# A fused convolution, Fourier mixing and FFN kernel: parts of the convolution and of the FFN issued in other stages of the mixing

## The chip, the cores and the metric

The kernel runs on one core of one Trainium2 chip, as one program. The metric is the device time of one execution in microseconds; less is better. Three executions of the kernel before took 10711.68, 10723.89 and 10726.16 us, so its median is 10723.89 us.

The core has five engines, each with its own queue that it works off in order: TensorE (PE in the profile, with PEld for the loading of weights), VectorE (DVE), ScalarE (ACT), GpSimd (POOL) and SyncE (SP, which here only starts transfers). They meet through semaphores: an instruction that needs another engine's result waits at the head of its queue, and everything behind it waits too.

## The reference, cut to what matters

The input is 64 images of 96 channels and 56x56 pixels in fp32. Three parts follow each other.

```
# 1 convolution block, per image
out = silu(bn(expand_w @ x))                 # 1x1, 96 -> 192 channels
out = channel_shuffle(shift_groups(out))     # shifts by one pixel, a quarter of the channels each way
out = silu(merge_bn(bn(depthwise3x3(out)) + bn(out * id_w)))
se  = sigmoid(grouped(relu(grouped(mean(out)))))      # squeeze and excitation, one gate per channel
x   = silu(bn(proj_w @ (out * se)) + x)               # 1x1, 192 -> 96
# 2 mixing, t = x as 3136 tokens of 96
h = relu(bn(layernorm(t) @ w1.T))            # 96 -> 192
X = fft(h, axis=tokens)
xr, xi = relu(X.re*rd - X.im*id + rb), relu(X.im*rd + X.re*id + ib)
t = t + bn(ifft(xr + 1j*xi).real @ w2.T)
# 3 FFN; q_mul rounds to a float with 5 exponent and 2 mantissa bits, q_acc to 5 and 10 bits
h = relu(q_acc(q_acc(q_mul(layernorm(t)) @ q_mul(W1)) + q_mul(b1)))   # 96 -> 384
t = t + q_acc(q_acc(q_mul(h) @ q_mul(W2)) + q_mul(b2))
```

## The kernel before, in words

Everything of an image stays in on-chip memory; an image is 96 channels on partitions (two blocks of 48 with a gap, 112 in all) by 3136 pixels. The loop at the end of the kernel (L668 to L683) runs over images b. For each it drains one generator, `mixing(b)`, and beside it two others: `ffn(b - 1)` for the image before and `conv_block(b + 1)` for the next. The schedule is written by hand: each generator issues some instructions and yields a weight, and `weave` (L651) advances the side generators so that they have used a share of their total cost as large as the share of the main one (`ffn` up to 0.85 of it, `conv_block` over all of it). So instructions stand in every engine's queue in the order in which `weave` called for them.

The parts, by the name of the PSUM tile that a reader finds in the profile:

- `expand_a`, `expand_b` (L268, L278): 1x1 expansion on PE into ps_ea and ps_eb, SiLU on ACT into e_a (128 channels, 7 parts) and e_b (the other 64 as two half images on 128 partitions, 5 parts).
- `depthwise` (L301): nine taps on DVE, each one instruction over 128x1568 elements (L307 the first, L309 the other eight), three calls for a picture: two halves of e_a and one of e_b. They accumulate in d, a tile with a single buffer. Then SiLU on ACT with a sum (L328), the gate (L339 to L357: small matmuls ps_se, Relu, Tanh, and scaled projection weights pw), and the projection (L363 to L368): eight parts of three matmuls into ps_pj, SiLU on ACT into t. Last it loads the image after the next (L371).
- `deviations` (L374): the mixing's layernorm. Seven times ps_c, squares on ACT, ps_v, a scaling on DVE (L395) and a power of -1/2 on POOL (L396); two `spread`s (L398) turn the deviation into a row that is written into t by DMA, and the factors into rs_full. In `mixing` they come first and nothing of the mixing can run before them.
- `mixing` (L414), after that: ps_w1 (L435, eight groups, evacuated by DVE at L444), ps_f1 (L459, six groups, copied by ACT at L468), ps_f2 (L487 and L493, six groups; each needs two ACT instructions L507, four DVE instructions L508 and L509, a Relu on ACT L510 and `mirrored` on DVE L570), ps_w2 (L523, L524, four groups, ACT L527), ps_i1 (L537, three groups, ACT L544) and ps_i2 (L555, four groups, added to t by DVE at L565). These PSUM tiles share two buffers (pool psa); all the other PSUM tiles share four (psb).
- `ffn` (L575): seven `centre` steps (ps_n L586, squares on ACT L588, a sum and scaling on DVE L591 and L592, the power on POOL L593), each followed by `turn` (DVE xt L599, which waits for the power, then ps_x L604 and an fp8 copy on ACT L605); then 21 `hidden` steps (ps_h L612, ACT copy to fp16 L614, bias on DVE L615, cast to fp8 on POOL L616) and seven `result` steps (ps_o L623, ACT copy L625, DVE L626, POOL adds t L628, SP writes the output L630).

t has two buffers, so image b + 1's projection writes the buffer from which `ffn(b - 1)` reads; x, with its own two buffers, is read by the expansion and by the projection.

Of the kernel before, what the change touches and what calls it, by code (L numbers as in the profile page):

```python
# [16 lines left out]
HW = 56  # L17
# [5 lines left out]
RPC = 8  # L23
# [11 lines left out]
def conv_attn_ffn(  # L35
# [265 lines left out]
    def depthwise(dst, e, r0, h):  # L301
        for n, tap in enumerate((4, 0, 1, 2, 3, 5, 6, 7, 8)):
            dy, dx = divmod(tap, 3)
            win = e[:, dy + r0 : dy + r0 + HH, dx : dx + HW]
            w = taps[:, h, tap : tap + 1]
            if n == 0:
                nc.vector.tensor_scalar(dst, win, w, None, ALU.mult)  # L307
            else:
                nc.vector.scalar_tensor_tensor(dst, win, w, dst, ALU.mult, ALU.add)  # L309
            yield 1.8 if n else 1.0  # L310

    def together(main, side):

        for w in main:
            yield w + next(side, 0.0)
        yield from side

    def conv_block(b):
        xi = x_buf[b % 2]
        tv = t_buf[b % 2][:, 0:NPIX].rearrange("p (b a) -> p b a", a=HW)  # L320

        d = work.tile([128, 3 * HH, HW], F32, tag="wide", name="d", bufs=1)
        sums = small.tile([128, 3], F32, tag="sums", name="sums")

        def mid_silu(i):
            dst = d[:, i * HH : (i + 1) * HH, :]
            h = i // 2
            nc.scalar.activation(dst, dst, AF.Silu, bias=mid_b[:, h : h + 1], accum_out=sums[:, i : i + 1])  # L328

        yield from together(depthwise(d[:, 0:HH], e_a, 0, 0), expand_b(b))  # L330
        mid_silu(0)
        yield from depthwise(d[:, HH:HW], e_a, HH, 0)
        mid_silu(1)
        yield from together(
            depthwise(d[:, HW : 3 * HH], e_b, 0, 1), expand_a(b + 1) if b + 1 < NB else iter(())
        )
        mid_silu(2)
        yield 2.0
# [10 lines left out]
        for h in range(2):  # L349
            nc.tensor.matmul(ps[:, h : h + 1], lhsT=ep_w[:, h, :], rhs=red, start=True, stop=True)  # L350
        for h in range(2):

            nc.scalar.activation(gate[:, h : h + 1], ps[:, h : h + 1], AF.Tanh, bias=ep_bh[:, h : h + 1], scale=0.5)
        nc.vector.tensor_scalar(gate, gate, 0.5, 0.5, ALU.mult, ALU.add)
        pw = small.tile([128, 3, CP], F32, tag="pw", name="pw", bufs=1)
        nc.vector.tensor_scalar(pw[:, 0, :], pj_w[:, 0, :], gate[:, 0:1], None, ALU.mult)
        nc.vector.tensor_scalar(pw[:, 1:3, :], pj_w[:, 1:3, :], gate[:, 1:2], None, ALU.mult)  # L357
        yield 1.0
        for j in range(HW // PJ):
# [4 lines left out]
            nc.tensor.matmul(ps, lhsT=pw[:, 0, :], rhs=d[:, r0 : r0 + PJ, :], start=False, stop=False)  # L364
            nc.tensor.matmul(  # L365
                ps, lhsT=pw[:, 1 + half, :], rhs=d[:, HW + rb : HW + rb + PJ, :], start=False, stop=True
            )
            nc.scalar.activation(tv[:, :, r0 : r0 + PJ], ps.rearrange("p a b -> p b a"), AF.Silu, bias=pj_sh)  # L368
            yield 0.5
# [4 lines left out]
    def deviations(b):  # L374
# [37 lines left out]
        return squares, variances, spread  # L412

    def mixing(b):  # L414
        t = t_buf[b % 2]
        squares, variances, spread = deviations(b)
# [9 lines left out]
        yield 1.5  # L426

        for g, (d, j0, n) in enumerate(
# [13 lines left out]
            if g == 0:  # L442
                spread(16, 12)
# [8 lines left out]
            yield 0.15 * n  # L452

        for g in range(C // 16):
# [17 lines left out]
            yield 2.0  # L472

        last = None
        for par, pq, k0, n in (
# [38 lines left out]
            yield 1.2  # L514
        mirrored(*last)

        for k0 in range(0, NK, 8):
# [10 lines left out]
            yield 3.0  # L528

        for g in range(3):  # L530
# [14 lines left out]
            yield 2.5  # L545

        for g in range(4):
# [18 lines left out]
            yield 1.0  # L566
# [8 lines left out]
    def ffn(b):  # L575
# [5 lines left out]
        def centre(g):  # L581
# [6 lines left out]
            nc.scalar.activation(sq, cen[:, :, 0:C], AF.Square)  # L588
            v = small.tile([CP, 4], F32, tag="v2", name="v2")
# [6 lines left out]
        def turn(g):  # L596
            cen, rs = held.pop(g)
# [3 lines left out]
            )  # L601
            ps = psb.tile([C, 8, HW], F32, tag="psb", name="ps_x")
# [4 lines left out]
        def hidden(j, m):  # L607
# [7 lines left out]
            nc.vector.tensor_scalar(y16, y16, qb1[:, m : m + 1], 0.0, ALU.add, ALU.max)  # L615
            nc.gpsimd.tensor_copy(held[j][:, m, :], y16, saturate=False)  # L616

        def result(j):
            h8 = held.pop(j)
            rows = slice(j * RPC, (j + 1) * RPC)  # L620
# [4 lines left out]
            nc.scalar.copy(o16, ps.rearrange("p (a b) -> p a b", b=HW))  # L625
            nc.vector.tensor_scalar(o16, o16, qb2, None, ALU.add)  # L626
# [8 lines left out]
        for g in range(NJ // 4 + 1):  # L635
            if g < NJ // 4:
                centre(g)
                yield 0.7
            if g:
                turn(g - 1)  # L640
                yield 0.6
        for j in range(NCH + 1):
            for m in range(3):
                if j < NCH:
                    hidden(j, m)
                    yield 0.4
                if m == 1 and j:
                    result(j - 1)
                    yield 0.3

    def weave(main, total, sides):  # L651
# [3 lines left out]
        for w in main:  # L655
            at += w / total
            for i, (side, cost, lo, hi) in enumerate(sides):
                goal = cost * min(1.0, (at - lo) / (hi - lo))
                while done[i] < goal:
                    step = next(side, None)  # L660
                    done[i] = cost if step is None else done[i] + step
# [5 lines left out]

    with tc.manual_schedule():  # L668
        if NB > 1:
            load_x(1)  # L670
        for _ in expand_a(0):
            pass
        for _ in conv_block(0):
            pass
        for b in range(NB):
            sides = []
            if b:
                sides.append((ffn(b - 1), 19.6, 0.0, 0.85))
# [174 lines left out]
```

## Time and profile before

| | |
|---|---|
| median of three runs | 10723.89 us |
| the profiled execution's own time | 10724.89 us |
| its span, first to last instruction | 10723.1 us |
| instructions | 262959 |
| mean granted TensorE clock | 0.856 of full speed |
| read from and written to HBM | 82.67 MB and 77.07 MB, 15 GB/s |

The profile was taken by the hardware on one execution. A group line gives the line of the code, the engine, the operation, tiles written and read with their shape, the number of instructions, their busy time in us and the mean of one in ns, and the idle time of the engine just before them with what ended it. A line of waits reads: engine and waiting line, what released it, then the total in us, how often, and the longest. A line of the timeline gives start and duration in us, the instruction, and in brackets the idle time before it. Matmuls overlap in PE, so a busy PE is not one at its peak; an fp32 matmul appears as two instructions. The granted clock (PEclk) is 1.00 at full speed and 0.5 at half; a mean lies between. The depthwise taps are the costliest DVE work, and the POOL casts of the FFN cost it most time:

```profile
L309 DVE SCALAR_TENSOR_TENSOR d<-e_a,taps,d 128x1568 f32<-128x1568 f32 x1024 | 1907.0, 1862 | 0.7
L616 POOL CAST h<-y 128x448 fp8e5<-128x448 f16 x1344 | 1589.4, 1193 | 1992.4 <-DVE y L615 1972.7
```

### The profile page before, as it was taken

What the parts mean: (1) busy time and instruction counts of PE and PEld (TensorE: products, weight loads), DVE (VectorE), ACT (ScalarE), POOL (GpSimd) and SP (SyncE); (2) the same over time, 40 slices, a digit from 0 to 9 for tenths busy, and PEclk for the clock granted to TensorE, in tenths of its full rate; (3) what the DMA queues carried; (4) which work ended last, traced back from release to release, by engine and by line L of the source; (5) the groups of instructions that cost most, each with busy time, mean ns of one, the idle gap of its engine ahead of it and who ended that gap; (6) DMA issues with size and microseconds to landing.
All of it is one profiled execution on the core that took longest, in us unless ns stands there. A gap on an engine that the chain in (4) does not pass through costs nothing. (4 is left out here: it accounts for less than half of the span.)

```text
span 10723.1 us, 262959 instructions
## 1 busy us (share of the span) xinstructions
PE 8726.5 (81%) x118530; PEld 6595.5 (62%) x118530; DVE 6560.7 (61%) x9035; ACT 4142.9 (39%) x7691; POOL 4211.8 (39%) x2704
## 2 busy tenths in 40 slices
PE   6888888888888888888888888887888888888787
PEld 4666666666666666665666656666666566666665
DVE  6656566566565665655656656566565565665655
ACT  2334344343343433433434334344343343433433
POOL 1444344344443344433433444334443443344433
PEclk8888888888888888888888888888888888888887
DMA  2110110101101111011010110111101101011000
GB/s 38 13 18 15 16 19 13 17 15 16 19 15 16 18 13 18 15 16 19 13 17 15 16 18 14 16 18 13 18 15 16 19 13 17 15 16 18 15 11 15
DMA packets 411392, 177.45 MB, mean 17 GB/s; under 512 B 366194, under 2 KB 409706, under 8 KB 410010
## 3 DMA queue, kind: packets, MB, share of 16 engines
q1 hardware_dynamic: 408508, 155.59, 11.6%
q8 instruction: 930, 15.24, 0.6%
q10 hardware_dynamic: 1264, 3.53, 0.1%
q0 software_dynamic: 496, 1.50, 0.1%
q14 instruction: 194, 1.59, 0.1%
HBM read 82.67 MB, written 77.07 MB: 15 GB/s over the span
## 5 line engine op out<-in xcount | busy, mean ns | idle before, releaser
L593 POOL TENSOR_TENSOR rs<-v,mhalf 112x4 f32<-112x4 f32 x448 | 987.3, 2204 | 3802.6 <-DVE v L592 3600.6
L616 POOL CAST h<-y 128x448 fp8e5<-128x448 f16 x1344 | 1589.4, 1193 | 1992.4 <-DVE y L615 1972.7
L309 DVE SCALAR_TENSOR_TENSOR d<-e_a,taps,d 128x1568 f32<-128x1568 f32 x1024 | 1907.0, 1862 | 0.7
L487 PE MATMUL ps_f<-l_tab,buf_g 128*128 128x112 f32 x3712 | 667.2, 353 | 605.4 <-DVE ue L509 604.7
L628 POOL TENSOR_TENSOR o<-t,o 112x448 f32<-112x448 f32 x448 | 941.6, 2102 | 430.6 <-DVE o L626 333.3
L309 DVE SCALAR_TENSOR_TENSOR d<-e_b,taps,d 128x1568 f32<-128x1568 f32 x512 | 1070.0, 2090 | 5.0
L487 PEld LDWEIGHTS ps_f<-l_tab,buf_g 128*128 128x128 f32 x3712 | 616.2, 258 | 705.9 <-issue 693.1
L435 PE MATMUL ps_w<-w1c,t 112*64 112x96 f32 x14336 | 1029.3, 327 | 3.2 <-DMA t<-dev_t 1.7
L435 PEld LDWEIGHTS ps_w<-w1c,t 112*64 112x64 f32 x14336 | 955.5, 197 | 40.9 <-issue 21.6
L591 DVE TENSOR_REDUCE v<-sq 112x4 f32<-112x384 f32 x448 | 247.0, 551 | 1177.8 <-ACT sq L588 1177.7
L523 PE MATMUL ps_w<-w2a,buf_h 128*112 128x96 f32 x3712 | 785.9, 299 | 144.6 <-DVE ue L509 144.6
L615 DVE TENSOR_SCALAR y<-y,qb 128x448 f16<-128x448 f16 x1344 | 646.9, 496 | 397.7 <-ACT y L614 384.1
L459 PE MATMUL ps_f<-f_tab,buf_h 128*64 128x58 f32 x24576 | 800.3, 224 | 81.5 <-DVE buf_h L444 81.5
L459 PEld LDWEIGHTS ps_f<-f_tab,buf_h 128*64 128x64 f32 x24576 | 749.8, 138 | 159.6 <-DVE buf_h L444 91.9
L523 PEld LDWEIGHTS ps_w<-w2a,buf_h 128*112 128x112 f32 x3712 | 610.1, 209 | 334.9 <-issue 226.6
L396 POOL TENSOR_TENSOR rs<-v,mhalf 112x4 f32<-112x4 f32 x448 | 705.8, 1579 | 253.8 <-DVE v L395 247.3
L368 ACT ACTIVATE t<-ps_pj,pjbn_b 112x392 f32<-112x392 f32 x512 | 316.5, 618 | 1241.3 <-PE ps_pj L365 1241.3
L524 PE MATMUL ps_w<-w2b,buf_h 128*112 128x96 f32 x3712 | 760.9, 292 | 0.0
L565 DVE SCALAR_TENSOR_TENSOR t<-ps_i,bn2c_b,t 112x392 f32<-112x392 f32 x512 | 296.7, 621 | 742.0 <-PE ps_i L555 742.0
L605 ACT CAST xq<-ps_x 96x448 fp8e5<-96x448 f32 x448 | 238.0, 531 | 1260.2 <-PE ps_x L604 1260.2
L623 PE MATMUL ps_o<-h,q 128*112 128x448 fp8e5 x1344 | 449.1, 428 | 317.6 <-POOL h L616 314.8
L444 DVE SCALAR_TENSOR_TENSOR buf_h<-ps_w,rs_full 128x768 f32<-128x768 f32 (+1 forms) x512 | 436.9, 854 | 423.4 <-PE ps_w L435 423.3
(159 smaller groups left out, 15841.9 us busy)
## 6 DMA issues: line engine op xcount, KB each, us to landing
x<-in_x SPq DMA_DIRECT2D x128, 588.0 KB, 8.4
out_dram<-o SPq DMA_DIRECT2D x896, 84.0 KB, 1.9
l_tab<-in_tab_l ACTq DMA_DIRECT2D x1, 1624.0 KB
r_tab<-in_tab_r ACTq DMA_DIRECT2D x1, 1568.0 KB
t<-dev_t SPq DMA_DIRECT2D x64, 7.0 KB, 1.8
t<-dev_t SPq DMA_DIRECT2D x64, 5.2 KB
ex_row_p<-in_expand_row POOLq DMA_DIRECT2D x1, 336.0 KB, 4.3
s_p<-in_bn POOLq DMA_DIRECT2D x1, 288.0 KB, 3.7
```

What stands on the lines that cost most here:

```text
L309: nc.vector.scalar_tensor_tensor(dst, win, w, dst, ALU.mult, ALU.add)
L396: nc.gpsimd.tensor_tensor(rs[:, js], v[:, js], mhalf[0:CP, 0:4], ALU.pow)
L435: nc.tensor.matmul(ps[hc * 64 : hc * 64 + 64, k, 0:C], lhsT=t[:, n0 : n0 + 64], rhs=w1c[:, hc * C : hc * C + C], start=True, stop=True,)
L459: nc.tensor.matmul(ps[r * 64 : r * 64 + 64, k, 0 : 2 * NK], lhsT=buf_h[:, n0 : n0 + 64], rhs=f_tab[:, r, :], start=True, stop=True,)
L487: nc.tensor.matmul(ps[:, k, 0:CP], lhsT=g_v[:, k1, 0:128], rhs=l_tab[:, k1, :], start=True, stop=True)
L523: nc.tensor.matmul(ps[:, k, 0:C], lhsT=pq_a[:, k1, :], rhs=w2a, start=True, stop=False)
L524: nc.tensor.matmul(ps[:, k, 0:C], lhsT=pq_b[:, k1 - u * (NS - 1), :], rhs=w2b[:, u, :], start=False, stop=True)
L593: nc.gpsimd.tensor_tensor(rs, v, mhalf[0:CP, 0:4], ALU.pow)
L615: nc.vector.tensor_scalar(y16, y16, qb1[:, m : m + 1], 0.0, ALU.add, ALU.max)
L616: nc.gpsimd.tensor_copy(held[j][:, m, :], y16, saturate=False)
L623: nc.tensor.matmul(ps, lhsT=q2[:, m, :], rhs=h8[:, m, :], start=m == 0, stop=m == 2)
L628: nc.gpsimd.tensor_tensor(o32, tv[:, rows, :], o16, ALU.add)
```

## The change

Four things change. `conv_block` is cut into `expand`, `depthwise_first` (both halves of e_a), `depthwise_last` (e_b), `excitation` and `project`, and each part gets a stretch of the mixing of its own, some of them one image further ahead; `conv_start`, called by `depthwise_first`, allocates d (still with a single buffer) and the sums, `excitation` is yielded in four steps of weight 1.0 and `project` in eight of 1.0. `deviations(b + 1)` runs as a side of image b's mixing, with its two `spread`s, so `mixing` begins with ps_w1. In the FFN each step is cut into smaller ones that are issued one stage apart: `centre`, `deviation`, `normalise` and `turn` on four groups in turn, `first`, `bias`, `quantise`, `second` and `result` on hidden chunks in turn. The cast to fp8 of the hidden layer (L616 before) is an ACT copy instead of a POOL one. The weights that `mixing` yields are other numbers (in the diff's order those of ps_w1, ps_f1, ps_f2, ps_w2, ps_i1 and ps_i2), and `weave` takes stretches on the scale of these weights: ps_w1 ends at 16.0, ps_f1 at 32.0, ps_f2 at 62.0, ps_w2 at 80.0, ps_i1 at 92.0 and ps_i2 at 112.0.

```
+    def expand(b):
+        if b < NB:
+            yield from expand_a(b)
+            yield from expand_b(b)
+
+    def depthwise(cv, i):
...
+            yield 1.8 if n else 1.0
+        nc.scalar.activation(dst, dst, AF.Silu, bias=mid_b[:, h : h + 1], accum_out=cv.sums[:, i : i + 1])
+
+    def depthwise_first(b, cvs):
+        if b < NB:
+            cvs[b] = conv_start(b)
+            yield from depthwise(cvs[b], 0)
+            yield from depthwise(cvs[b], 1)
+
+    def depthwise_last(b, cvs):
+        if b < NB:
+            yield from depthwise(cvs[b], 2)
...
-        squares, variances, spread = deviations(b)
...
-            yield 0.15 * n
+            yield 0.286 * n
-            yield 2.0
+            yield 2.67
-            yield 1.2
+            yield 5.0
-            yield 3.0
+            yield 4.5
-            yield 2.5
+            yield 4.0
-            yield 1.0
+            yield 5.0
...
-            nc.gpsimd.tensor_copy(held[j][:, m, :], y16, saturate=False)
+            held["y", i] = y16
+        def bias(i):
+            y16 = held["y", i]
+            nc.vector.tensor_scalar(y16, y16, qb1[:, i % 3 : i % 3 + 1], 0.0, ALU.add, ALU.max)
+        def quantise(i):
+            nc.scalar.copy(held[i // 3][:, i % 3, :], held.pop(("y", i)), saturate=False)
...
+        for g in range(ng + 3):
+            if 2 <= g < ng + 2:
+                normalise(g - 2)
+            if g < ng:
+                centre(g)
+            if 1 <= g < ng + 1:
+                deviation(g - 1)
+            yield 1.3
+            if 2 <= g < ng + 2:
+                turn(g - 2)
+        n = 3 * NCH
+        for i in range(n + 5):
+            if i < n:
+                first(i)
+            if 1 <= i <= n:
+                bias(i - 1)
+            yield 0.4
+            if 2 <= i <= n + 1:
+                quantise(i - 2)
+            j, m = divmod(i - 5, 3)
+            if i >= 5 and m == 0 and j < NCH:
+                second(j)
+            if i >= 6 and m == 1 and j < NCH:
+                result(j)
+            yield 0.1
...
-                sides.append((ffn(b - 1), 19.6, 0.0, 0.85))
-                sides.append((conv_block(b + 1), 58.2, 0.0, 1.0))
-            weave(mixing(b), 65.9, sides)
+            weave(
+                mixing(b),
+                [
+                    (ffn(b - 1) if b else iter(()), 26.0, 0.0, 60.0),
+                    (depthwise_last(b + 1, cvs), 15.4, 0.0, 34.0),
+                    (excitation(b + 1, cvs), 4.0, 38.0, 50.0),
+                    (expand(b + 2), 3.6, 38.0, 62.0),
+                    (project(b + 1, cvs), 8.0, 62.0, 84.0),
+                    (depthwise_first(b + 2, cvs), 30.8, 70.0, 112.0),
+                    (deviations(b + 1), 13.2, 85.0, 105.0),
+                ],
+            )
```

A side is given as generator, total cost, and the stretch over which that cost is spent. Ahead of the loop stand, one after another, `expand(0)`, `depthwise_first(0)`, `depthwise_last(0)`, `excitation(0)`, `expand(1)`, `project(0)`, `depthwise_first(1)` and `deviations(0)`.

## The prediction

> **What bounds the kernel now.** I read the page's first part, then the busy time by stage, then the waits, then the instructions in order of time. First the page: no engine is full.
>
> ```profile
> PE 8726.5 (81%) x118530; PEld 6595.5 (62%) x118530; DVE 6560.7 (61%) x9035; ACT 4142.9 (39%) x7691; POOL 4211.8 (39%) x2704
> ```
>
> TensorE (PE) is idle for 10723 - 8727 = 1997 us, 31 us of each of the 64 images. From the first ps_w1 matmul of image 1 (290.7 us) to that of image 62 (10411.5) are 61 images: 165.9 us each. The windows of image 31, cut at the first matmul of each stage (ps_c, ps_w1, ps_f1, ps_f2, ps_w2, ps_i1, ps_i2), show what each stage leans on:
>
> ```profile
> core 0: us, PE busy (x) PEld busy (x) DVE busy (x) ACT busy (x) POOL busy (x), PEclk, DMA share, GB/s
> 5238.90:5267.50 28.60, 23.15 (x202) 14.55 (x202) 15.30 (x26) 9.54 (x21) 18.78 (x11) 0.95 0.53 41
> 5267.50:5294.90 27.40, 22.65 (x264) 20.71 (x264) 16.90 (x20) 5.08 (x10) 4.95 (x2) 0.68 0.01 1
> 5294.90:5309.70 14.80, 14.80 (x402) 13.04 (x403) 11.34 (x14) 8.71 (x19) 8.37 (x6) 1.00 0.01 3
> 5309.70:5341.10 31.40, 19.82 (x147) 14.71 (x146) 24.45 (x37) 16.35 (x25) 10.76 (x7) 0.76 0.04 12
> 5341.10:5364.60 23.50, 21.97 (x174) 16.53 (x178) 19.84 (x27) 12.60 (x26) 14.04 (x11) 0.89 0.06 15
> 5364.60:5379.00 14.40, 9.39 (x405) 7.80 (x397) 8.82 (x9) 6.96 (x12) 9.64 (x6) 0.88 0.15 40
> 5379.00:5404.60 25.60, 24.93 (x273) 16.44 (x273) 5.33 (x11) 5.36 (x10) 0.00 (x0) 0.93 0.03 6
> ```
>
> PE comes closest to full in every stage except ps_f2, where it is busy 19.8 of 31.4 us and VectorE (DVE) 24.5. ScalarE (ACT) is far from full everywhere. The waits name the chain in ps_f2:
>
> ```profile
> PE ps_f L487 <- DVE ue L509: 604.7, 192, 4.7
> PE ps_x L604 <- DVE xt L599: 490.8, 322, 4.3
> ACT ue L507 <- DVE ue L509: 754.7, 384, 2.7
> ```
>
> One group of it that no depthwise tap interrupts:
>
> ```profile
> 5336.59 0.72 ACT L507 ACTIVATE ue<-ps_f,fa 128x448 f32<-128x448 f32 x1 [0.51 <-DVE buf_h L570]
> ...
> 5338.07 0.68 DVE L509 SCALAR_TENSOR_TENSOR ue<-ps_f,fa,ue 128x448 f32<-128x448 f32 x1
> 5338.79 0.72 ACT L507 ACTIVATE ue<-ps_f,fa 128x448 f32<-128x448 f32 x1 [1.47 <-DVE ue L509]
> 5339.55 0.68 DVE L508 SCALAR_TENSOR_TENSOR s<-ps_f,fa,ue 128x448 f32<-128x448 f32 x1 [0.79 <-ACT ue L507]
> 5340.26 0.95 ACT L510 ACTIVATE s<-s 128x896 f32<-128x896 f32 x1 [0.75 <-DVE s L508]
> ```
>
> From the first ACT instruction to the end of the last are 4.62 us (5336.59 to 5341.21), and ACT idles 2.2 of them. Whatever ACT must do besides stands before or after this chain in its queue.
>
> The granted clock matters too. The same 16 matmuls take twice as long after a pause:
>
> ```profile
> 5309.68 1.95 PE L487 MATMUL ps_f<-l_tab,buf_g 128*128 128x112 f32 x16
> 5317.41 3.73 PE L487 MATMUL ps_f<-l_tab,buf_g 128*128 128x112 f32 x16 [3.61 <-DVE ue L509]
> ```
>
> **The change, by stages of the new order.** I read which steps each stage now issues from the weights in the diff and from the built queues, and price them by rows of before at full clock. "Behind another" means back to back: two ACT copies of 448 take 0.99 us, so 0.44 for one more.
>
> *ps_f2.* Of the FFN's 21 hidden steps 19, of its fp8 casts all 21, and all 7 outputs now fall here (before: 4 y copies in this window), with the 12 copies of expand and the last SiLU of the depthwise part. The casts move from POOL (L616, 25.2 us in this image) to ACT. An fp16-to-fp8 cast of 128x448 on ACT is in no row; the ends are 0.20 (64x56, L297) and 0.95 (128x896, L510, from SBUF as here); I take 0.44, by the y copies of equal size (0.55 alone). ACT over the first five groups: chains 4 x 4.62 + 4.3 = 22.8; 19 y + 21 casts + 6 o at 0.44 = 20.2; 10 expand copies 4.5; SiLU 1.8 (1.60 and its accumulator 0.19); Relu and two Tanh 0.7. That is 50.0 us. At the end of a step ACT also waits for PE, which has to get through that step's expansion (from start to start 0.87 us for a ps_ea, 1.23 for a ps_eb) before the next group (1.9): 3.7 in the second step, 1.9 in the fourth, 0.9 in the fifth. With 2.0 for the first group: **58.5 us**. The sixth chain lies beside PE's next work. DVE has some 35 us here and is not the bound.
>
> *ps_w2 and the projection*, now together: PE, in a row: second layer 0.75, two expansions 1.7, eight parts of ps_pj at 2.0 (six matmuls at 0.33), 29 frequencies of ps_w2 at 0.40, one group of ps_i1 1.8: **32 us**. ACT's copies lie beside it. DVE has nothing to do.
>
> *Depthwise taps for image b+2.* The buffer d is single, and in the built queue the first tap waits for the last ps_pj matmul (PE's count of the last projection). So DVE, idle for those 32 us, begins only now: 16 taps at 1.87 (eight of them take 14.98 us from 54.54 on) and two first taps at 1.07 are 32.1 us. Queued in order between them, and so late by them: 7 variances and 2 dev (1.5) and eight evacuations of ps_i2 (4.6). The evacuations of groups 2 and 3 wait in turn for PE, which waits for dev behind taps: after dev, ps_dev 0.28, ps_rs 0.47, one ps_v 0.83 and 28 matmul pairs of ps_i2 1.75, 3.5 us, and 2.7 at the second. Sum: **44.4 us**. PE has only 24 us there.
>
> *ps_w1.* DVE still: six evacuations at 0.95 and two at 0.55 (6.8), 5 taps (8.5), four reduces with their scalings (2.9), three xt (1.7), less 0.4 of overlap: **19.5**. The first xt stands one evacuation behind the value that POOL's pow (1.0 us) needs; some tenths.
> *ps_f1.* PE: 6 x 2.04, one ps_n 0.9, four turns 1.3, two ps_h 0.5, and 0.75 until the last copy releases ps_f2: **15.8**.
>
> Sum 58.5 + 32 + 44.4 + 19.5 + 15.8 = **170 us an image** at full clock, against 165.9.
>
> *Clock.* Before, only the waits of 3 to 4 us in ps_f2 and ps_w1 cost clock (0.76, 0.68). Now PE waits 4 us and more in each of five steps of ps_f2, and for the taps that follow the projection. What a slow group adds is between 0 and 3.73 - 1.95 = 1.8 us; for five steps 0 to 9, for four bursts among the taps and ps_w1 0 to 7. I take half, 8: **178 us**.
>
> The Trainium skill, "TensorE: Matmul & The Clock Gate", "HAM oscillation — how this bites in real kernels", says that an idle gap longer than a window of about 3.4 us makes the next burst begin at half clock, and that a busy window releases it. The 3.73 beside 1.95 us after a wait of 3.61 agrees. An estimate by that page alone would be 1.7 us lost in each of nine bursts, 15 us, and 185 us an image. It speaks against gathering PE's work into bursts as this change does.
>
> *Costed at nothing:* deviations one image ahead (their PE and ACT work lies beside the taps; without that cover 14: ps_c and ps_v 11.6, the spreads 2.4); POOL's pow and o32, and SP's 18 transfers an image (POOL is 39% busy; the dev rows land in 1.8 us, ahead of their ps_w1). That PE no longer waits for xt in ps_x (490.8 / 64 = 7.7 us) is a gain that the sum holds already: in ps_w1 DVE is late next.
>
> *Ends.* Image 0: expand of image 1 (12 us), 18 taps and the deviations stand alone ahead of the first ps_w1, which moves from 144 to 180; its mixing without FFN 136, so ps_w1 of image 1 at 316 (before 290.7). Image 62 without taps 147, image 63 without convolution 112, the last FFN 42 (before 58, 10665 to 10723). Total 617 + 61 x 178 = 11,475 us against 10,723.1 of span; the profiled run took 10,724.89, the median of the three 10,723.89, so nothing is added.
>
> **The rivals.**
> *PE packed: faster.* The stages' other engines keep up, and the waits for ue, xt, h, dev and red (604.7 + 144.6 + 490.8 + 314.8 + 97.3 + 62.8 = 1715 us) go, because every producer is now a step ahead: 10,724 - 1715 + 25 = 9,030. For it: its matmuls, start to start while the clock was 1, need only 118 us an image. Against it: ACT's 50 us in ps_f2, and d. It decides if ps_f2 stays under 54 us with the taps not waiting for the projection; both must hold.
> *Same phases at full clock:* 617 + 61 x 170 = 10,990. For it: the clock was 1.00 in ps_f1 and 0.95 in ps_c.
> *ACT without overlap, half clock throughout:* each y and cast at 0.55, 4.4 us more, and 15 us of clock: 189 us an image, 12,150.
> *The change does not do what it says*, since its parts meet another limit at the same price: 165.7 us an image would be no change.
>
> **How the numbers follow.** Forecast 11,470, chance 0.45; full clock 0.26; the worse case 0.17; packed 0.12. Between 165.4 and 166.0 us an image lies "within 0.2%" (about what a measurement of this kernel can tell from no change); I give it 0.03, out of the lower flank of the full-clock case and the upper one of packed, and faster keeps 0.12, slower 0.85. The range 10,650 to 12,150 takes in the cast's ends (0.24 less or 0.51 more for 21 casts: 5 us less, 11 more an image, so 165 from the full-clock sum and 189 from the forecast) and leaves out packed and the upper half of the worse case.
>
> **What would show it.** Right: ps_f2 the longest stage, 55 to 70 us, with ACT over 70% busy there; the first tap L326 idle some 30 us <- PE ps_pj L382; DVE over 85% busy from there to ps_f1; PE under 80%. A cast on ACT near 0.5. Wrong: ps_f2 under 45 us, or taps that start beside ps_w2, or PE over 88% busy; then the packed case holds. A clock of 0.9 or more would point to the full-clock case.

## The result and the profile after

The changed kernel takes 12,082.67 us (median of four runs, 12,063.0 to 12,109.0) against 10,725.02 us for the one before in the same comparison: a ratio of 1.127, with a 95% interval of 1.1247 to 1.1294. It is slower by an eighth. The forecast was 11,470 us; the sign and the place of the loss were right, its size was little more than half of what came (the profiled span is 12,078.1 us, 1,355 more than before; the forecast span of 11,475 was 752 more).

The page's first part, for all engines:

```profile
PE 9221.3 (76%) x118530; PEld 6620.5 (55%) x118530; DVE 6473.8 (54%) x9035; ACT 4846.2 (40%) x9035; POOL 1925.3 (16%) x1360
```

Every engine but ACT (39% before) is now busy for a smaller share, and the number of matmuls is the same while PE is busy 495 us longer: its mean granted clock went from 0.856 to 0.800. From the first ps_w1 of image 1 (337.7 us) to that of image 62 (11,756.3) are 187.2 us an image, before 165.9. The windows of image 31, cut at the first matmul of ps_w1, ps_f1, ps_f2, ps_w2, ps_i1 and ps_i2 (columns as in the prediction's windows):

```profile
5953.63:5977.36 23.73, 19.36 (x287) 17.54 (x285) 23.11 (x29) 5.99 (x11) 5.56 (x4) 0.89 0.01 2
5977.36:5992.12 14.76, 14.60 (x411) 13.56 (x411) 9.33 (x13) 7.67 (x17) 4.49 (x3) 1.00 0.01 3
5992.12:6066.88 74.76, 48.37 (x310) 23.49 (x311) 35.01 (x65) 44.61 (x84) 8.17 (x6) 0.75 0.05 15
6066.88:6090.24 23.36, 23.36 (x153) 17.57 (x151) 1.23 (x4) 7.22 (x13) 1.80 (x1) 1.00 0.04 9
6090.24:6107.67 17.43, 14.30 (x423) 10.34 (x422) 13.20 (x8) 5.56 (x8) 0.00 (x0) 0.94 0.88 72
6107.67:6137.30 29.63, 21.00 (x276) 17.76 (x275) 18.53 (x24) 4.58 (x10) 10.40 (x7) 0.67 0.01 2
```

In ps_f2, 75 us long and 31 before, no engine is full: PE 48, ACT 45 and DVE 35 us. In ps_w2 PE is full and DVE idle; in ps_i2 PE and DVE are both far from full, at a clock of 0.67. So the loss lies in stages where engines take turns. The turns can be read in the chain of waits over ps_f2 of image 31 (first the share of each line, then some pieces in order of time: start, us, what held the chain):

```profile
by line: PE ps_ea L274 14.0%; PE ps_eb L287 11.7%; issue 10.2%; DVE s L525 8.9%; ACT ue L524 8.6%; ACT h L648 8.1%; PE ps_f L504 6.9%; PE ps_f L510 6.9%; DVE ue L526 4.5%; ACT y L640 3.5%; PE ps_o L654 3.5%; PE ps_h L638 3.2%; DVE d L328 2.
...
6015.21 1.01 PE ps_se L357 x4
6016.22 4.38 PE ps_ea L274 x24
6020.60 1.98 PE ps_f L504 x16
6022.61 0.73 ACT ue L524
...
6029.73 3.15 PE ps_ea L274 x16
6032.87 2.02 PE ps_f L510 x28
```

The expansion of a coming image stands in PE's queue ahead of the next ps_f2 group, so ACT's next chain cannot start before it is through. Behind the projection a second ring shows in the timeline (start, us, instruction, idle time before it and its releaser):

```profile
6094.23 1.04 DVE L326 TENSOR_SCALAR d<-e_a,taps 128x1568 f32<-128x1568 f32 x1 [26.11 <-PE ps_pj L382]
...
6128.75 3.73 DVE L328 SCALAR_TENSOR_TENSOR d<-e_a,taps,d 128x1568 f32<-128x1568 f32 x2
6132.40 0.17 DVE L417 TENSOR_TENSOR dev<-v,rs 112x12 f32<-112x12 f32 x1
6132.71 0.53 PE L419 MATMUL ps_dev<-eye,dev 112*12 112x112 f32 x2 [5.09 <-DVE dev L417]
6133.17 1.03 PE L426 MATMUL ps_rs<-rs,sel 112*128 112x12 f32 x4
6134.13 3.24 PE L572 MATMUL ps_i<-r_tab,buf_h 64*64 64x56 f32 x56
6137.42 1.16 DVE L582 SCALAR_TENSOR_TENSOR t<-ps_i,bn2c_b,t 112x392 f32<-112x392 f32 x2 [4.86 <-PE ps_i L572]
```

The first tap waits 26 us for the last projection, as forecast. Later two taps (3.73) hold back `dev` behind them, PE waits 5.09 us for it, then does ps_dev, ps_rs and ps_i2 at half clock (3.24 at a granted clock of 0.50, against 1.84 at 1.00 for as many matmuls at 6114.97), DVE waits 4.86 us for that, and the next taps wait behind the add. PE and DVE work one after the other.

### The profile page after: what moved, and what is told of

Its sections match the earlier page's. It is cut to its first block, busy times and chain, and to the rows that moved or that the text cites. A ratio compares the mean times of both kernels' runs of the same rounds, so it can differ in the third digit from the quotient of the medians.

```text
span 12078.1 us, 263414 instructions
## 1 busy us (share of the span) xinstructions
PE 9221.3 (76%) x118530; PEld 6620.5 (55%) x118530; DVE 6473.8 (54%) x9035; ACT 4846.2 (40%) x9035; POOL 1925.3 (16%) x1360
## 4 chain that ended last, share of the span: by engine, by line
PE 59%; DVE 23%; ACT 9%; issue 7%; POOL 2%; DMA 0%; POOLq 0%; ACTq 0%; DVEq 0%
DVE d L328 10%; PE ps_f L476 6%; PE ps_i L572 6%; PE ps_ea L274 6%; PE ps_eb L287 5%; DVE s L525 4%; ACT ue L524 3%; PE ps_v L411 3%; ACT h L648 3%; PE ps_w L541 3%; PE ps_pj L380 3%; PE ps_w L540 3%; PE ps_c L402 3%; PE ps_f L504 3%; PE ps_pj L381 3%
## 5 line engine op out<-in xcount | busy, mean ns | idle before, releaser
L328 DVE SCALAR_TENSOR_TENSOR d<-e_a,taps,d 128x1568 f32<-128x1568 f32 x1024 | 1894.0, 1850 | 25.2
L664 POOL TENSOR_TENSOR o<-t,o 112x448 f32<-112x448 f32 x448 | 636.5, 1421 | 4637.8 <-DVE o L662 4635.8
L413 POOL TENSOR_TENSOR rs<-v,mhalf 112x4 f32<-112x4 f32 x448 | 640.4, 1436 | 3322.2 <-DVE v L412 3037.6
L525 DVE SCALAR_TENSOR_TENSOR s<-ps_f,fa,ue 128x448 f32<-128x448 f32 (+1 forms) x512 | 327.4, 639 | 1436.2 <-ACT ue L524 1436.2
L326 DVE TENSOR_SCALAR d<-e_a,taps 128x1568 f32<-128x1568 f32 x128 | 132.4, 1035 | 1647.4 <-PE ps_pj L382 1644.6
L614 POOL TENSOR_TENSOR rs<-v,mhalf 112x4 f32<-112x4 f32 x448 | 638.3, 1425 | 2160.4 <-DVE v L613 2160.4
L454 PEld LDWEIGHTS ps_w<-w1c,t 112*64 112x64 f32 x14336 | 701.8, 153 | 208.6 <-DVE buf_h L461 180.0
L572 PE MATMUL ps_i<-r_tab,buf_h 64*64 64x56 f32 x14336 | 778.5, 299 | 1.0 <-ACT buf_h L561 1.0
L648 ACT CAST h<-y 128x448 fp8e5<-128x448 f16 x1344 | 755.9, 568 | 0.0
L411 PEld LDWEIGHTS ps_v<-mean_m,sq 96*112 96x112 f32 x3584 | 586.9, 246 | 304.1 <-issue 159.1
L572 PEld LDWEIGHTS ps_i<-r_tab,buf_h 64*64 64x64 f32 x14336 | 735.8, 210 | 5.9 <-ACT buf_h L561 1.2
L640 ACT CAST y<-ps_h 128x448 f16<-128x448 f32 x1344 | 712.3, 536 | 27.1 <-PE ps_h L638 0.6
L274 PE MATMUL ps_ea<-x,ex_w 112*32 112x448 f32 x3584 | 687.0, 925 | 1.0 <-ACT gate L361 1.0
```

What stands on the lines that cost most here:

```text
L274: nc.tensor.matmul(ps[qs], lhsT=ex_w[:, qs], rhs=window(xi, q, j * RPC, RPC), start=True, stop=True)
L411: nc.tensor.matmul(var[:, k : k + 1], lhsT=sq[:, k, :], rhs=mean_m, start=True, stop=True)
L454: nc.tensor.matmul(ps[hc * 64 : hc * 64 + 64, k, 0:C], lhsT=t[:, n0 : n0 + 64], rhs=w1c[:, hc * C : hc * C + C], start=True, stop=True,)
L525: nc.vector.scalar_tensor_tensor(s[:, q, 0:n, :], im, par[:, m : m + 1], a, ALU.mult, ALU.add)
L572: nc.tensor.matmul(ps[pr, bk, k, 0:HW], lhsT=buf_h[pr, n2 * 48 : n2 * 48 + 64], rhs=r_tab[pr, n2, :], start=True, stop=True,)
L640: nc.scalar.copy(y16, ps)
```

## The experiments

All lengths of stages below are means over images 4 to 59, from the first matmul of one stage to the first of the next; the column ps_i2 holds what follows until the next ps_w1. The column "image" is the distance from the first ps_w1 of image 1 to that of image 62, divided by 61.

| kernel | ps_w1 | ps_f1 | ps_f2 | ps_w2 | ps_i1 | ps_i2 | image |
|---|---|---|---|---|---|---|---|
| before | 27.4 | 14.8 | 31.4 | 23.7 | 14.4 | 54.3 | 165.9 |
| before + new FFN steps (b1_ffn) | 21.0 | 15.9 | 31.8 | 25.2 | 13.2 | 52.7 | 159.8 |
| the same + ACT casts (c1_cast_steps) | 20.7 | 16.5 | 35.8 | 25.4 | 12.8 | 52.3 | 163.4 |
| after with POOL casts (e1_pool) | 23.9 | 15.2 | 68.4 | 23.4 | 18.4 | 31.5 | 180.7 |
| after | 23.9 | 15.0 | 74.8 | 23.4 | 18.3 | 31.8 | 187.2 |
| after, expansions moved (d1_expand) | 23.7 | 18.6 | 62.0 | 28.7 | 19.0 | 30.2 | 182.1 |
| after, FFN and projection late (c3_late) | 20.5 | 17.9 | 64.6 | 16.2 | 17.6 | 61.1 | 197.8 |

### The first four: casts, the tile d, the clock, the buffers of y16

The theory at that point was the prediction's: ACT's queue bounds ps_f2, the late release of d bounds what follows, and PE's clock adds to both.

**e1_pool**, the cast back on POOL:

```
-            nc.scalar.copy(held[i // 3][:, i % 3, :], held.pop(("y", i)), saturate=False)
+            nc.gpsimd.tensor_copy(held[i // 3][:, i % 3, :], held.pop(("y", i)), saturate=False)
```

> The changed kernel with the fp8 cast of the hidden layer on POOL again, nothing else undone. Theory (in ps_f2 ACT's queue is the bound, and each cast costs it 0.6 us because the next y copy waits for it): 21 casts less, some 11 us of ACT work, of which the steps that end on PE's expansion give back a part; ps_f2 from 75 to 66 us, 8 us an image, 11,580 us (11,450 to 11,700). Rival (ps_f2 is long because PE runs its bursts at half clock): only 2 to 3 us an image, 11,900. A second rival (the cast on POOL was a good part of the time before, since it is slow beside the DVE taps): slower than 12,083.

Measured: 11,700.05 us, ratio 1.0896 (1.0857 to 1.0935). 383 us less, 6.5 us for each image by the table, at the upper edge of what the theory allowed; ps_f2 fell from 74.8 to 68.4 us and no other stage by more than 0.3. The casts on ACT cost 6.5 us an image in that stage, and most of the loss is elsewhere.

**e2_split**, d as three tiles, so that the first taps wait for the fourth part of the projection and not for the eighth:

```
-        cv.d = work.tile([128, 3 * HH, HW], F32, tag="wide", name="d", bufs=1)
+        cv.d = {}
...
+        cv.d[i] = work.tile([128, HH, HW], F32, tag=f"wide{i}", name="d", bufs=1)
+        dst = cv.d[i]
```

> The changed kernel with d as three tiles (two halves of e_a's part, one for e_b's) in place of one, so that the first nine taps of image b+2 wait for the fourth part of the projection instead of the eighth. Theory (DVE's 26 us of idling for the projection, and the taps that then push everything behind them, set the time from there to ps_f1): taps start 15 us earlier, beside ps_w2; PE becomes the bound beside ps_i2 for the last 2 to 3 of these; 12 to 13 us an image less, 11,300 us (11,150 to 11,450). Rival (PE at half clock is the bound there anyway): under 3 us an image, 11,900 or more.

Measured: 12,012.43 us, ratio 1.1187 (1.1154 to 1.1219). The theory fell, and the time lies where the rival put it (11,900 or more). The tap did start earlier; its wait in total went from 1644.6 us to this:

```profile
DVE d L327 <- PE ps_pj L382: 670.7, 63, 19.7
```

and in the timeline of one image it is 10.5 us, for 26.1 before the edit:

```profile
6046.31 1.04 DVE L327 TENSOR_SCALAR d<-e_a,taps 128x1568 f32<-128x1568 f32 x1 [10.53 <-PE ps_pj L382]
```

From the first ps_f2 to the first tap are 86.6 us in place of 102.1, but from that tap to the next ps_w1 61.0 in place of 46.2. The taps ran ahead by eight and then stood in DVE's queue behind the first variance, which needs t whole (5.5 us in this image), and after that the ring went on as before. So VectorE's 32 us of taps were not what set that stretch.

**e3_warm**, which adds 100 matmuls an image: in five of the 21 hidden steps, one for each of five ps_f2 groups, the ps_h matmul is issued 21 times in place of once, with the same operands and into the same tile:

```
+            for _ in range(21 if i in (2, 7, 11, 15, 20) else 1):
```

> The changed kernel with 20 more copies of one ps_h matmul in the first hidden step of each of five ps_f2 groups, into the same tile with the same result: 100 matmuls, some 20 us of PE work an image more at full clock, placed where PE waits for ACT's chain. Theory (what ps_f2 takes over the 58 us of its sum is half clock after these pauses): the granted clock in ps_f2 goes from 0.74 to 0.9 or more, the bursts ps_f2 and ps_ea run at full speed, and ps_f2 gets 6 to 10 us shorter although PE does more: 11,560 us (11,400 to 11,750). Rival (the clock is not what lengthens the bursts): ps_f2 stays or gets longer by what does not fit in the pauses, 12,080 to 12,500 us.

Measured: 11,789.07 us, ratio 1.0979 (1.0944 to 1.1013), mean clock 0.864 in place of 0.800. The added work made the kernel 294 us faster: ps_f2 69.3 us in place of 74.8 although PE is busy 59.5 us there in place of 48.4, with the clock in that stage at 0.90 in place of 0.74. So the clock is shown to be a part of what lengthens ps_f2. A little over half of what the theory expected came: the added matmuls also take time on the path, and in image 31 ps_h holds 21.1% of the chain of waits over this stage.

**e4_y16**, five buffers of y16 in place of three:

```
-            y16 = work.tile([128, CH], F16, tag="y16", name="y16", bufs=3)
+            y16 = work.tile([128, CH], F16, tag="y16", name="y16", bufs=5)
```

> The changed kernel with five y16 buffers instead of three. With three, the y copy of step i writes the buffer that the cast just ahead of it in ACT's queue reads, so the two do not overlap (1.03 us a pair instead of 0.88). Theory (ACT is the bound in ps_f2): 19 times 0.15, 2.5 to 3 us an image less, 11,900 us. Rival (PE's bursts end each step): no difference, 12,060 to 12,110 us.

Measured: 12,042.13 us, ratio 1.1214 (1.1182 to 1.1247), 40 us less, 0.5 us an image. The pair of copy and cast did get faster, as the theory said: one y now begins 0.89 us after the last one, 1.03 before the edit.

```profile
6001.60 0.54 ACT L640 CAST y<-ps_h 128x448 f16<-128x448 f32 x1
...
6002.49 0.55 ACT L640 CAST y<-ps_h 128x448 f16<-128x448 f32 x1
```

But ps_f2 is 74.5 us in place of 74.8, where the theory wanted 2.5 to 3 us: time saved in ACT's queue is hardly time saved in the stage, so ACT alone is not the bound there.

### The parts of the change alone

**b1_ffn**: the kernel before, with the new FFN generator (the cast still on POOL) over 0 to 0.85 of the mixing as it was.

```
-                sides.append((ffn(b - 1), 19.6, 0.0, 0.85))
+                sides.append((ffn(b - 1), 26.0, 0.0, 0.85))
```

> The kernel before with the new FFN steps alone: centre, deviation, normalise, turn and first, bias, quantise, second, result each one step apart, the cast still on POOL, the FFN still spread over 0 to 0.85 of the mixing and the convolution as it was. In the profile of before PE waits 490.8 us ahead of ps_x for DVE's xt and 317.6 us ahead of ps_o for POOL's h; the theory that the FFN steps are sound and only their place (all before two thirds of the mixing, most of them beside ps_f2) is harmful expects a part of these 808 us to go: 10,300 to 10,700 us. The rival, that steps held one apart keep PSUM buffers longer and put a new wait in, expects 10,800 us or more.

Measured: 10,343.68 us, ratio 0.9645 (0.9631 to 0.966). **This part alone is 3.5% faster than the kernel before**, and it is the fastest version found. The waits of PE:

```profile
PE ps_o L637 <- POOL h L631: 304.3, 197, 4.2
PE ps_x L612 <- DVE xt L603: 6.6, 7, 1.8
```

The 490.8 us ahead of ps_x are gone; of the 314.8 for POOL's h ahead of ps_o 304.3 are left. ps_w1 fell from 27.4 to 21.0 us, as much as the whole gain of an image (165.9 to 159.8): the stage whose clock was 0.69 before now has 0.84.

**b2_cast**: the kernel before, with the casts on ACT and nothing else.

```
-            nc.gpsimd.tensor_copy(held[j][:, m, :], y16, saturate=False)
+            nc.scalar.copy(held[j][:, m, :], y16, saturate=False)
```

> The kernel before with the casts of h on ScalarE alone. Undoing them in the changed kernel gave 383 us, 6.2 us per image. Theory: that price is owed to the place, ScalarE being the engine of the ps_f2 stage there; in the even spreading of before ScalarE is 40% busy and has room, so the move costs nothing or gains a part of the 317.6 us for which PE waits for POOL's h: 10,600 to 10,800 us. Rival: 21 x 0.57 us of ScalarE time per image are paid wherever they stand, at about the same 6 us per image: 11,000 us or more.

Measured: 11,261.04 us, ratio 1.0501 (1.0483 to 1.0518). The theory that the move is free where ACT has room fell. The wait is this one:

```profile
ACT h L616 <- DVE y L615: 973.8, 1344, 3.0
```

All 1344 casts wait at the head of ACT's queue for DVE's maximum of the same step, 15.2 us an image, and everything queued behind waits with them. An image takes 174.1 us, 8.2 more than before; the time is the rival's (11,000 or more), and c1_cast_steps below tells whether its reason holds too. ACT was 39% busy and had no room in the sense that counts.

**b3_conv**: the changed kernel with the old FFN steps and POOL casts over 0 to 60, that is the new places alone: those of the convolution, of the deviations, and the shorter stretch of the FFN.

```
-                    (ffn(b - 1) if b else iter(()), 26.0, 0.0, 60.0),
+                    (ffn(b - 1) if b else iter(()), 19.6, 0.0, 60.0),
```

> The changed kernel with the old FFN steps (hidden with its three operations in one step, POOL cast, result a step behind), in the same window of 0 to 60; so the new places of the convolution parts and of the deviations are left alone. Theory: the packing of the FFN beside the chains of ps_f2 and the taps behind the last projection are what cost, not the new steps: 11,600 to 12,000 us, near the 11,700 of the changed kernel with POOL casts or worse, since the old steps wait for DVE and POOL within a step. Rival: the new steps are the harm, and with the old ones the time falls under 11,300 us.

Measured: 13,287.28 us, ratio 1.2388 (1.2363 to 1.2413), worse than the theory allowed, and the rival is out: the new steps save 1,587 us in these places (13,287 to 11,700). The old steps packed into half of the mixing wait within themselves:

```profile
PE ps_x L621 <- DVE xt L616: 930.2, 315, 7.9
```

The new places are what costs, and they cost more with the old steps.

**b4_dev**: the changed kernel with the deviations back at the start of their own mixing and the other windows moved back by 13.2.

```
     def mixing(b):
         t = t_buf[b % 2]
+        yield from deviations(b)
...
-                    (deviations(b + 1), 13.2, 85.0, 105.0),
```

> The changed kernel with the deviations put back at the start of their own mixing (13.2 of cost ahead of ps_w1, all other windows moved back by 13.2), the rest as it is. Theory, formed on the traces of the changed kernel and of the split tile: behind the last projection DVE and PE take turns in a ring at half clock (two taps 3.73 us, dev 0.17, its PE work 0.53 and 1.03, ps_i2 3.24, the add 1.16, the taps again: near 10 us for one of four groups), because the deviations are issued between the taps and ps_i2. Without them ps_i1 to the end of ps_i2 should fall from 50.1 to 38 to 42 us, the taps of the last part move beside the deviations, and the deviations cost 8 to 18 us of their own at the start: 11,600 to 12,200 us in all, with the fall in ps_i1 and ps_i2 as the test. Rival: DVE's 32 us of taps alone set that stretch; it stays at 46 us or more and the whole is 12,400 or more.

Measured: 12,952.37 us, ratio 1.2076 (1.2052 to 1.21), beyond the theory's range; both halves of the theory went further than it said. From the first ps_i1 to the end of the last ps_i2 are 29.7 us in place of 50.2: without the deviations the ring is gone, and DVE is busy there for 25.9 of 30.2 us. But the deviations at the start take 39.6 us. The two windows of one image, the deviations (first ps_c to first ps_w1), and ps_i1 to the end of ps_i2, and two rows of the first:

```profile
6345.20:6384.20 39.00, 29.51 (x119) 22.37 (x118) 18.32 (x29) 8.29 (x17) 13.13 (x10) 0.54 0.00 1
6516.40:6546.60 30.20, 19.52 (x616) 17.62 (x615) 25.89 (x18) 5.66 (x7) 0.00 (x0) 0.75 0.50 42
...
6354.95 1.60 ACT L330 ACTIVATE d<-d,mid_b 128x1568 f32<-128x1568 f32 x1 [18.12 <-DVE d L328]
...
6357.13 1.65 PE L411 MATMUL ps_v<-mean_m,sq 96*112 96x1 f32 x8 [8.56 <-ACT sq L404]
```

At a clock of 0.54 PE's small matmuls need 30 of the 39 us. For another 8.6 it waits for taps that the shorter stretch left over: four of them run on behind the last ps_i2 with two adds, ACT's SiLU waits for them, and the deviations' squares stand behind it. From the first ps_i1 to the next ps_w1 it is 69.2 us, 50.2 in the changed kernel. So in the surroundings that this change makes, deviations one image ahead are worth 870 us, though they build the ring.

### What is left: the cast in the new steps, buffers, windows, expansions

**c1_cast_steps**: b1_ffn with the casts on ACT.

```
-            nc.gpsimd.tensor_copy(held[i // 3][:, i % 3, :], held.pop(("y", i)), saturate=False)
+            nc.scalar.copy(held[i // 3][:, i % 3, :], held.pop(("y", i)), saturate=False)
```

> The kernel before with the new FFN steps (10,344 us) and the casts on ScalarE as well: the whole change but for the convolution and the deviations. Where the cast was moved alone, in the old steps, ScalarE waited 973.8 us for DVE's y ahead of it, since the cast was issued right behind the copy and the maximum of its own step. With the new steps the cast comes a step later and that wait should be near nothing. Theory: what is left of the price is ScalarE's own 0.57 us where ps_f2's chains run through it, 8 or so casts per image, 3 to 5 us, less what the taps gain that no longer run beside POOL: 10,300 to 10,600 us. Rival: the price of the move is 6 to 8 us per image wherever the cast stands: 10,730 to 10,850 us.

Measured: 10,569.8 us, ratio 0.9866 (0.985 to 0.9883), inside the theory's range. With the cast a step later the wait for DVE is gone, and the price is 3.6 us an image (159.8 to 163.4): 4.0 more in ps_f2 (31.8 to 35.8) and a little less elsewhere.

**c2_y16_steps**: b1_ffn with five buffers of y16, the edit of e4_y16.

> The kernel before with the new FFN steps, POOL casts, and five buffers of y16 in place of three. In that kernel's trace ScalarE waits 261.7 us ahead of y for POOL's cast (the buffer that it is to fill is still being read) and PE 142.2 us ahead of ps_h for ScalarE's y. Theory: those waits stand in ScalarE's queue ahead of ps_f2's ue and ps_w2's copies, and a part goes: 10,200 to 10,320 us. Rival: they lie under PE's or DVE's time: within 0.2% of 10,344 us.

Measured: 10,358.51 us, ratio 0.9667 (0.9653 to 0.9682), no different from b1_ffn. ACT's 261.7 us of waiting for POOL's cast are gone from its waits, and PE's wait for h has grown from 304.3 to 372.6 us: the rival holds, the wait moved to the next reader.

**c3_late**: e1_pool with other windows.

```
-                    (ffn(b - 1) if b else iter(()), 26.0, 0.0, 60.0),
+                    (ffn(b - 1) if b else iter(()), 26.0, 0.0, 81.0),
-                    (project(b + 1, cvs), 8.0, 62.0, 84.0),
-                    (depthwise_first(b + 2, cvs), 30.8, 70.0, 112.0),
-                    (deviations(b + 1), 13.2, 85.0, 105.0),
+                    (project(b + 1, cvs), 8.0, 82.0, 98.0),
+                    (depthwise_first(b + 2, cvs), 30.8, 84.0, 112.0),
+                    (deviations(b + 1), 13.2, 98.0, 111.0),
```

> The changed kernel with POOL casts (11,700 us) and wider windows: the FFN over 0 to 81 in place of 60, so that nearly half of its hidden steps move from ps_f2 to ps_w2, the projections over 82 to 98 (beside ps_i1 and ps_i2, out of ps_w2), the taps over 84 to 112, the deviations over 98 to 111. Theory: the stretch behind the last projection is a floor of some 45 us by itself (taps 32, adds 4.6, waits of the ring), so that later projections lengthen ps_i1 to ps_i2 by 13 to 18 us and ps_f2 gains 8 to 12 and ps_w2 2: 11,600 to 12,100 us. Rival: the crowding of the FFN beside ps_f2 is the whole loss, and the time falls under 11,300 us.

Measured: 12,722.38 us, ratio 1.1871 (1.1848 to 1.1895), beyond the theory's range on the slow side. ps_w2 fell by 7.2 us and ps_f2 by only 3.8; ps_i1 and ps_i2 together grew by 28.8 us: 15.6 up to the end of the last ps_i2, inside the theory's 13 to 18, and 13.0 behind it, where the last steps of the deviations now stand between ps_i2 and the next ps_w1. The theory had left these out. The timeline shows how the deviations came to be late:

```profile
6447.61 1.60 ACT L330 ACTIVATE d<-d,mid_b 128x1568 f32<-128x1568 f32 x1 [16.53 <-DVE d L328]
...
6449.21 0.95 ACT L404 ACTIVATE sq<-ps_c 96x448 f32<-96x448 f32 x2
6449.79 1.65 PE L411 MATMUL ps_v<-mean_m,sq 96*112 96x1 f32 x8 [15.88 <-ACT sq L404]
```

The SiLU of the depthwise part stands in ACT's queue ahead of the deviations' squares and waits 16.5 us for nine taps; so the squares wait, and PE waits 15.9 us for them with ps_i2 queued behind. That the crowding of ps_f2 is the whole loss is out as well.

**d1_expand**: the changed kernel with the expansions out of ps_f2.

```
-                    (expand(b + 2), 3.6, 38.0, 62.0),
+                    (expand_a(b + 2) if b + 2 < NB else iter(()), 2.1, 6.0, 32.0),
+                    (expand_b(b + 2) if b + 2 < NB else iter(()), 1.5, 62.0, 80.0),
```

> The changed kernel with the expansions taken out of ps_f2: expand_a over 6 to 32 (beside ps_w1 and ps_f1), expand_b over 62 to 80 (beside ps_w2), the rest as it is. In the changed kernel's chain of waits over one ps_f2 stage (77 us, image 31) the expand matmuls on PE hold 14.0% (ps_ea) and 11.7% (ps_eb), together some 19 us at half clock, each between a group's last ps_o and the next group's ps_f2: the prediction had counted 6.5 us of waits for PE there, and took ScalarE's queue for the bound. Theory: they are on the path, and ps_f2 falls by 14 to 20 us; ps_w1 and ps_f1 grow by 3 to 7 us and ps_w2 by 6 to 8, since PE or DVE is busy there: 6 to 9 us per image less, 11,500 to 11,720 us. Rival: ScalarE bounds ps_f2 as predicted, the expand matmuls hide beside its queue, ps_f2 falls only by the 5 us of their copies, and with the growth elsewhere the time is 12,000 us or more.

Measured: 11,770.28 us, ratio 1.0962 (1.0941 to 1.0984), 312 us less and 50 us above the theory's range; the rival (12,000 or more) is out. ps_f2 fell by 12.9 us, ps_f1 grew by 3.6 and ps_w2 by 5.4. The window of its ps_f2 in image 31 shows why not the whole 19 us came back:

```profile
5840.40:5902.80 62.40, 37.50 (x191) 25.11 (x192) 35.88 (x68) 39.63 (x74) 8.46 (x7) 0.67 0.06 17
```

With less to do PE was granted less clock (0.67 there, 0.75 before the edit), so what remained ran slower: 16 ps_f2 matmuls (L504) hold the chain for 3.70 and 3.26 us here, 1.98 in the pieces shown above. The edit also takes the expansions' 12 copies from ACT's queue in this stage; in the chain of the changed kernel none of them appears.

## Why the prediction was right, and where its sizes failed

**The direction** came from the new places of the parts, as forecast. By the runs: the new FFN steps alone take 379 us off, ACT casts on top of them put 226 on, and the new places 1,356 more with POOL casts (10,344 to 11,700) or 1,513 with ACT casts (10,570 to 12,083). The gain that the change could have brought is in it, and it is given back by the places. By stage, from b1_ffn to e1_pool, ps_f2 grew by 36.6 us an image and the stretch of ps_i1 and ps_i2, which lost the projections and part of the deviations, gave back only 16.0; the other stages add 0.4. Work moved into a stage costs its own length where engines take turns, and frees little where PE was busy anyway.

That the time fell inside the stated range (10,650 to 12,150) owes something to luck: its upper end was reached with a dearer cast on ACT, and what lengthened the kernel was mostly something else, as the pieces show.

**The 170 us at full clock, by piece.** The prediction's sum can be set beside the trace:

| piece | predicted, full clock | measured |
|---|---|---|
| first ps_f2 to first tap | 58.5 + 32 = 90.5 | 102.1 |
| first tap to the next ps_w1 | 44.4 | 46.2 |
| ps_w1 | 19.5 | 23.9 |
| ps_f1 | 15.8 | 15.0 |
| sum | 170.2 | 187.2 |

*ps_f2, 58.5 us* is the step that failed most: it took ACT for the bound, with 6.5 us of waits for PE (3.7, 1.9 and 0.9). Up to the end of the sixth group's matmuls, which the sum stands for, image 31 took 70.5 us. The stage is a ring of all three engines. In image 31 the chain of waits gives the expansion matmuls 14.0% (ps_ea) and 11.7% (ps_eb) of the 75 us, some 19 us, and d1_expand, which moved them, shortened the stage by 12.9 us. Of the signs named, the one on ACT was wrong: 44.6 of 74.8 us is 60%, not over 70%, and the stage is longer than the 55 to 70 us given. The parts of ACT's own queue were near: the sum's 50.0 us hold five chains with 2.2 us of idling each, so some 39 us of work, 41 with the sixth chain, and 44.6 were measured. A cast on ACT was assumed at 0.44 us back to back and "near 0.5"; the groups of the changed kernel say

```profile
L648 ACT CAST h<-y 128x448 fp8e5<-128x448 f16 x1344 | 755.9, 568 | 0.0
L640 ACT CAST y<-ps_h 128x448 f16<-128x448 f32 x1344 | 712.3, 536 | 27.1 <-PE ps_h L638 0.6
```

In the timeline a y and a cast begin 1.03 us after the last pair (0.88 in the sum), which over 19 pairs is 2.9 us. With two more buffers of y16 the pair came down to 0.89 (e4_y16), and the stage lost only 0.3 us: ACT's sum was not what the stage's length followed. DVE's share was right (35.0 us, "some 35").

*Projection and ps_w2, 32 us*: right (31.6 in image 31, from the end of the sixth group's matmuls to the first tap), and right in its kind (PE full, clock 1.00, DVE idle; over the whole span PE is at 76%, under the 80 given), and with it the wait of the first tap (26.1 us in image 31; "some 30").

*Taps, 44.4 us*: right as a time to the next ps_w1 (46.2), but another 4.9 us of the ring's last round in image 31 (an add and two taps, 1.16 and 3.73) fall behind its first matmul, into ps_w1's 23.9, so the stretch was short by 6.7; without them ps_w1 is 19.0 against 19.5. And DVE was not its owner. DVE is busy 79% of the time from the first tap to ps_f1, not over 85%; e2_split gave it 15.5 us more of lead and the end did not move; b4_dev took the deviations away and the stretch from ps_i1 to the end of ps_i2 fell from 50.2 to 29.7 us, with four taps left over. Deviations "at nothing" was wrong in that sense: they close the ring. It was the right place for them even so, since b4_dev paid 39.6 us in the old one. (Small slips that move nothing: the prediction's pieces after dev add up to 3.3 us and not 3.5, those of ps_f1 to 15.7 and not 15.8, and in the ps_i1 window of before POOL, at 9.64 us, is a little fuller than PE at 9.39.)

*Clock, 8 us*: too little. The sum of the misses is 17.0 us, and e3_warm took 5.0 of them back (182.2 us an image) by added work alone. The trace cannot share out the rest between clock and turns: a ring at half clock is both. The Trainium skill's "TensorE: Matmul & The Clock Gate", "HAM oscillation — how this bites in real kernels", from which the prediction had an estimate of 185 us, came closer than the prediction's own halving; the measured value is 187.2, and the 3.24 against 1.84 us for 56 matmuls in the timeline above, the first in a ring with pauses of 3.54 and 5.09 us, agree with its rule that a burst after a pause longer than some 3.4 us starts at half clock. At 6107.67 a pause of 3.13 us (the stop described at the end) was enough for a clock of 0.50. The half that the prediction took had no row behind it.

*Ends*: 617 predicted, 12,078 - 61 x 187.2 = 659 measured. With 61 x (187.2 - 178) = 561 these 42 us make up the 603 us between the forecast span and the measured one.

**The rivals.** PE packed needed ps_f2 under 54 us and taps that do not wait; neither held. The full clock did not come. The case of ACT without overlap and half clock throughout gave 189 us an image, and its number is nearest to the measured one, though its mechanism (ACT's pair at 1.1 us) is only part: ps_w2 and ps_f1 ran at full clock.

**Open** is how much of the 12 us that ps_f2 exceeds its forecast by would be left at full clock, how much of the loss belongs to each of the new places (the expansions alone were worth 312 us, the deviations gain, and no run spread the FFN alone over a longer stretch), and whether the new places could be made to pay with fewer turns; moving the FFN and the projection later (c3_late) did not do it, and no further set of windows was run.

## What to carry to other kernels

Read from the chain of waits, not from busy shares, whether a stage belongs to one engine or to engines that take turns: in a ring an added instruction can cost time on whichever engine it stands (casts of 12 us on ACT cost 6.5 here, expansions of 19 us on PE 12.9), and a head start for one engine (e2_split) or a faster queue on one (e4_y16) moves little. Cutting a chain into steps issued one apart gained 3.5% by itself, while gathering work into stages of its own cost 13% on top of that (10,344 to 11,700), in part because bursts and pauses cost TensorE its clock (a mean of 0.878 in b1_ffn, 0.822 in e1_pool). Before moving an operation to a "free" engine, look at what it will wait for there: the same cast cost 8.2 us an image right behind its producer's step and 3.6 a step later.

## What the hardware showed that was not expected

- Added matmuls made the kernel faster: 100 more an image took 294 us off, the mean clock going from 0.800 to 0.864.
- GpSimd's work and VectorE's taps slow each other. In b1_ffn's timeline the same cast takes 2.04 us beside a tap and 0.55 us where no tap runs; the taps over e_b took 2.35 us there on average, 2.09 in the kernel before, and 1.85 in b2_cast, where the casts are on ScalarE. The cast is not all of it: in c1_cast_steps, with the casts on ScalarE too, they took 1.96.

```profile
5122.94 2.04 POOL L631 CAST h<-y 128x448 fp8e5<-128x448 f16 x1 [13.72 <-DVE y L628]
...
5143.05 0.55 POOL L631 CAST h<-y 128x448 fp8e5<-128x448 f16 x1
```

- In the changed kernel TensorE stops in the middle of a ps_i1 group and waits for nothing that the profile shows, 168.5 us in 63 places, once an image (36.8 us before). It is the group that runs just after the next x has been asked for, while DMA is at 0.88 of its engines:

```profile
6099.16 1.77 PE L554 MATMUL ps_i<-inv_tab,buf_g 112*32 112x56 f32 x125
...
6104.06 0.29 PE L554 MATMUL ps_i<-inv_tab,buf_g 112*32 112x56 f32 x3 [3.13 <-issue]
```

  It lies beside the taps here. That the load is the cause was not tried.
